# The first layer's selective scan as 256 time steps, with the sequences on the partitions

## The chip, the cores and the metric

The kernel runs on one core of one Trainium2 chip. The metric is the device time of the whole kernel in microseconds. Most executions of a kernel agree within 0.3%. A core has five engines with their own programs: TensorE (PE in the profile, with its weight loads as PEld), VectorE (DVE), ScalarE (ACT), GpSimd (POOL) and SyncE (SP, which here only starts transfers).

## The reference, cut to what matters

Two images of 64x64 positions and 256 channels go through two layers. Only the first is changed. It runs a selective scan over each image along both axes and in both directions, so there are 2 x 64 = 128 sequences of 64 steps for each axis and direction:

```python
xz = x @ in_proj_w.T                      # 256 -> 2 x 512
xi, z = jnp.split(xz, 2, axis=-1)
xi = silu(causal_conv(xi, 4 taps) + conv_b)
dt, Bm, Cm = jnp.split(xi @ x_proj_w.T, [DT_RANK, DT_RANK + D_STATE], axis=-1)
dt = softplus(dt @ dt_w.T + dt_b)
dA = jnp.exp(dt[..., None] * A)           # 512 channels x 16 states
dBu = (dt * xi)[..., None] * Bm[:, :, None, :]
def step(h, t):
    h = dA_t * h + dBu_t
    return (h, jnp.einsum('ndk,nk->nd', h, C_t))
y = (ys + xi * Dp) * silu(z)
return y @ out_w.T
# ... both directions and axes, then one product with fc_w, and the residual
```

The second layer (another kind of scan, with group norm) follows and is the same in both kernels.

## The kernel before

The channels lie on the partitions. A block is four sequences in both directions, and each block of each of the 16 states costs one pass of the hardware's scan instruction:

```python
for n in range(NS0):                      # 16 states
    for c in range(CT):                   # four groups of 128 channels
        nc.scalar.activation(decs[:, c, :, 1:], dts[:, c, :, 1:], AF.Exp, scale=neg_a[:, c, n:n+1])
    nc.vector.tensor_mul(h, dtx, b_n)     # b_n: row B_n on every partition, by a matmul
    nc.vector.tensor_tensor_scan(hf, decay_flat, hf, 0.0, ALU.mult, ALU.add)
    nc.vector.tensor_mul(h, h, c_n)       # c_n likewise
    ...                                   # the next block's front, in pieces
    for c in range(CT):                   # y += h * C, summed in PSUM
        nc.tensor.matmul(y[:, c, :], lhsT=k.ident, rhs=h[:, c, :], start=False, stop=n == NS0 - 1)
```

All numbers are float32 (f32).

## Time and profile before

| | time before |
|---|---|
| median of 3 runs | 14784.51 us (14781.2 to 14787.17) |
| layer 0 (two images) | 10,560 us |
| layer 1 (two images) | 4206 us |
| VectorE busy in layer 0 | 91% (9621 of 10,560 us) |
| TensorE busy in layer 0 | 86% (9105 of 10,560 us) |

These are two groups of instructions of the kernel before, shape by shape: line, engine, operation, out<-in, size, count, then busy us and the mean ns of one record, then idle time before them.

```profile
L379 PE MATMUL ps_y<-h,ident 128*128 128x512 f32 x8192 | 4363.8, 682 | 1052.1 <-DVE h L372 1041.1
...
L614 PE MATMUL ps_tr<-ident,xh 128*128 128x128 f32 x1024 | 155.0, 274 | 0.0
```

L379 is the last line of the code above. The kernel issues 64 blocks x 16 states x 4 = 4096 such products, and the profile has 8192 records. L614, a transpose in layer 1, is issued 1024 times and has 1024 records. So an f32 product leaves two records, and a transpose one.

### The profile page before, as it was taken

The page shows a single profiled execution, that of the slowest core. Times are in us where ns is not written, and L with a number is a line of the kernel's source. Part 1 is how long each engine was busy: PE and PEld are TensorE (multiplying, and loading weights), DVE is VectorE, ACT ScalarE, POOL GpSimd, SP SyncE. Part 2 cuts the span into 40 slices and gives each one's busy share as a digit, 9 for nine tenths or more (in the row PEclk, how much of TensorE's full clock was granted, in tenths as well). Part 3 has the DMA queues.
Part 4 walks back from the last instruction along what each step waited for, and adds up shares of the span by engine and source line. Part 5 has one row for each costly group of instructions (what it writes and reads, how often), then busy time and mean ns, then how long its engine had stood idle before and what let it go on. Part 6 is the DMA issues. An engine that isn't in the chain of part 4 may idle for free.

```text
span 14766.4 us, 110663 instructions
## 1 busy us (share of the span) xinstructions
PE 12671.3 (86%) x44688; PEld 6607.1 (45%) x44688; DVE 11979.4 (81%) x8514; ACT 6025.9 (41%) x8637; POOL 968.2 (7%) x1070
## 2 busy tenths in 40 slices
PE   8888888888888878888888888888888888788888
PEld 3433343434333345656533433334344333456565
DVE  8999999899999965555589999998999999655555
ACT  4444444444444423333344444444444444233333
POOL 0000000000000011111200000000000000111112
PEclk9999999999999989999989999989999998899999
DMA  0000000000000000000000000000000000000000
GB/s 18 0 0 0 0 0 6 0 0 0 0 0 0 0 10 5 1 6 3 15 13 0 0 0 0 0 6 0 0 0 0 0 0 0 10 6 1 6 4 9
DMA packets 23553, 46.87 MB, mean 3 GB/s; under 512 B 6592, under 2 KB 15296, under 8 KB 21504
## 3 DMA queue, kind: packets, MB, share of 16 engines
q1 hardware_dynamic: 23040, 39.80, 0.8%
q8 instruction: 350, 5.73, 0.2%
q14 instruction: 163, 1.34, 0.0%
HBM read 31.40 MB, written 8.39 MB: 3 GB/s over the span
## 4 chain that ended last, share of the span: by engine, by line
DVE 59%; PE 29%; ACT 8%; issue 3%; DMA 0%; POOL 0%; DVEq 0%; SPq 0%; POOLq 0%; ACTq 0%
DVE h L369 26%; DVE h L368 13%; DVE h L372 12%; PE ps_y L379 5%; PE ps_mm L530 5%; PE ps_mm L687 4%; PE ps_mm L403 3%; PE ps_mm L558 3%; DVE xn L508 2%; PE ps_y L672 2%; PE ps_seg L642 2%; PE ps_y L348 2%; ACT rms L450 2%; PE ps_bc L332 1%; PE ps_mm L242 1%
## 5 line engine op out<-in xcount | busy, mean ns | idle before, releaser
L379 PE MATMUL ps_y<-h,ident 128*128 128x512 f32 x8192 | 4363.8, 682 | 1052.1 <-DVE h L372 1041.1
L360 ACT ACTIVATE decay<-dt,neg_a 128x504 f32<-128x504 f32 x4096 | 2615.2, 704 | 5525.1 <-DVE h L369 5522.7
L369 DVE TENSOR_TENSOR_SCAN h<-decay,h 128x2048 f32<-128x2048 f32 x1024 | 4530.0, 4424 | 88.6 <-ACT xc L290 1.4
L379 PEld LDWEIGHTS ps_y<-h,ident 128*128 128x128 f32 x8192 | 1710.8, 219 | 3578.2 <-issue 1832.2
L372 DVE TENSOR_TENSOR h<-h,ps_bc 128x2048 f32<-128x2048 f32 x1024 | 2342.0, 2287 | 118.0 <-PE ps_bc L332 33.5
L332 PE MATMUL ps_bc<-dbc,ident 48*128 48x512 f32 x4096 | 2146.1, 637 | 305.1 <-DVE h L368 305.1
L368 DVE TENSOR_TENSOR h<-dtx,ps_bc 128x2048 f32<-128x2048 f32 x1024 | 2333.1, 2278 | 12.0 <-PE ps_bc L332 11.4
L530 PE MATMUL ps_mm<-xn,w_in 128*128 128x256 f32 (+1 forms) x5120 | 1388.1, 406 | 181.1 <-DVE xn L508 85.0
L332 PEld LDWEIGHTS ps_bc<-dbc,ident 48*128 48x128 f32 x4096 | 681.5, 189 | 1624.8 <-issue 1240.4
L530 PEld LDWEIGHTS ps_mm<-xn,w_in 128*128 128x128 f32 (+1 forms) x5120 | 873.3, 184 | 663.5 <-DVE xn L508 231.2
L687 PE MATMUL ps_mm<-yg,w_out 128*128 128x256 f32 x2048 | 527.9, 403 | 274.7 <-DVE conv L544 265.2
L224 POOL TENSOR_SCALAR xn<-XU,gn_scale,gn_shift 128x256 f32<-128x256 f32 x128 | 85.2, 676 | 8949.3 <-PE ps_mm L242 7097.7
L544 DVE SCALAR_TENSOR_TENSOR conv<-ps_mm,cols,conv 128x252 f32<-128x252 f32 (+2 forms) x1536 | 663.3, 467 | 9.3
L450 ACT ACTIVATE rms<-ps_mm,eps_rms 128x256 f32<-128x256 f32 x256 | 121.4, 474 | 1167.8 <-PE ps_mm L558 1167.8
L242 PE MATMUL ps_mm<-xn,w_in 128*128 128x256 f32 x2048 | 567.7, 425 | 21.9 <-ACT xi L251 21.9
L687 PEld LDWEIGHTS ps_mm<-yg,w_out 128*128 128x128 f32 x2048 | 381.1, 196 | 428.5 <-DVE conv L544 319.7
L360 ACT ACT_TABLE_LOAD x420 | 538.9, 1283 | 7.6
L242 PEld LDWEIGHTS ps_mm<-xn,w_in 128*128 128x128 f32 x2048 | 410.5, 209 | 221.7 <-issue 108.3
L403 PE MATMUL ps_mm<-h,w_out 128*128 128x256 f32 x2048 | 475.9, 385 | 27.8 <-DVE h L393 27.0
L508 DVE TENSOR_TENSOR xn<-XU,rms 128x256 f32<-128x256 f32 x256 | 278.5, 1126 | 251.9 <-ACT rms L450 251.9
L273 PE MATMUL ps_mm<-xi,diag_w 128*128 128x252 f32 (+2 forms) x1536 | 467.3, 385 | 0.0
L450 ACT ACTIVATE sq<-yg 128x1024 f32<-128x1024 f32 x128 | 135.3, 1057 | 808.2 <-DVE yg L679 808.2
(131 smaller groups left out, 11758.8 us busy)
## 6 DMA issues: line engine op xcount, KB each, us to landing
XU<-in_x_dram SPq DMA_DIRECT2D x16, 512.0 KB, 7.1
out_dram<-Y SPq DMA_DIRECT2D x32, 256.0 KB, 2.4
w_in<-in_L_t_Win_dram SPq DMA_DIRECT2D x4, 1160.0 KB, 5.1
w_in<-in_L_b_Win_dram SPq DMA_DIRECT2D x4, 1160.0 KB, 7.8
w_in<-in_L_mh_in_w_dram SPq DMA_DIRECT2D x2, 1024.0 KB, 7.9
dt<-in_L_fc_w_dram SPq DMA_DIRECT2D x4, 512.0 KB, 5.9
w_in<-in_L_mv_in_w_dram SPq DMA_DIRECT2D x2, 1024.0 KB, 4.8
w_out<-in_L_t_Wout_dram SPq DMA_DIRECT2D x4, 512.0 KB, 4.9
```

Of the source, the lines that this page charges most:

```text
L242: nc.tensor.matmul(pp[:, j * TB : (j + 1) * TB], lhsT=w_in[:, kt, mt * P : (mt + 1) * P], rhs=xn[:, kt, :], start=kt == 0, stop=kt == KT - 1,)
L332: nc.tensor.matmul(pb, lhsT=k.ident[:NX, r : r + 1].to_broadcast([NX, P]), rhs=dbc, start=True, stop=True,)
L360: nc.scalar.activation(decs[:, c, :, 1:], dts[:, c, :, 1:], AF.Exp, scale=neg_a[:, c, n : n + 1],)
L368: nc.vector.tensor_mul(h, dtx, b_n)
L369: nc.vector.tensor_tensor_scan(hf, decay.rearrange("p c v -> p (c v)"), hf, 0.0, ALU.mult, ALU.add)
L372: nc.vector.tensor_mul(h, h, c_n)
L379: nc.tensor.matmul(y[:, c, :], lhsT=k.ident, rhs=h[:, c, :], start=False, stop=n == NS0 - 1,)
L403: nc.tensor.matmul(po[:, o * TB : (o + 1) * TB], lhsT=w_out[:, c, j, o * P : (o + 1) * P], rhs=yg[:, c, j * TB : (j + 1) * TB], start=c == ...
L508: nc.vector.tensor_mul(seqs(xn[:, kt, :]), us[:, kt], seqs(rms))
L530: nc.tensor.matmul(ps, lhsT=w_in[:, kt, col : col + width], rhs=xn[:, kt, :], start=kt == 0, stop=kt == KT - 1,)
L544: nc.vector.scalar_tensor_tensor(dsts[:, :, j:], pss[:, :, : L - j], w[:, TAPS - 1 - j : TAPS - j], dsts[:, :, j:], ALU.mult, ALU.add,)
L687: nc.tensor.matmul(po[:, o * TB : (o + 1) * TB], lhsT=w_out[:, c, o * P : (o + 1) * P], rhs=yg[:, c, :], start=c == 0, stop=c == CT - 1,)
```

## The change

The intent is to take the scan instruction, and the broadcasts of B and C, away. Both images together have 128 sequences for one axis and direction, so the sequences go on the partitions, and the kernel steps through time itself: 2 axes x 2 directions x 64 = 256 steps, in 64 blocks of 4 steps. I call the four steps of a block n0 to n3. B and C are then per-partition scalars. The states are handled in pairs. The core of the new step:

```diff
-                    nc.vector.tensor_mul(h, dtx, b_n)
-                    nc.vector.tensor_tensor_scan(
-                        hf, decay.rearrange("p c v -> p (c v)"), hf, 0.0, ALU.mult, ALU.add
-                    )
-                    nc.vector.tensor_mul(h, h, c_n)
+                    if s % 2 == 0:
+                        e = two.tile([P, 4, DI], F32, name="e")
+                        nc.gpsimd.tensor_mul(
+                            e, w["a_bc"][s // 2], dt.unsqueeze(1).to_broadcast([P, 4, DI])
+                        )
+                    a = ps_a.tile([P, 2, DI], F32, name="ps_a")
+                    act(a, e[:, 2 * (s % 2) : 2 * (s % 2) + 2, :], AF.Exp)
+                run_late()                               # y of the pair before, see below
+                    nc.vector.tensor_mul(a, a, h)
+                for j in range(2):
+                        nc.vector.scalar_tensor_tensor(
+                            h[:, j, :], dtx, b_n, a[:, j, :], ALU.mult, ALU.add
+                        )
+                late.append(lambda s=s: sum_y(s))
+                pieces(s)                                # one piece of other blocks' work
```

y needs h turned back to channels on partitions. Even states do it by a product, odd ones by scaling and a transpose that adds into PSUM:

```diff
+YROUTE = ("diag", "act") * (NS0 // 2)
+                    if kind == "diag":
+                        dg = dgp.tile([P, TS], F32, name="dg")
+                        act(dg, k.ident, AF.Copy, scale=c_n)          # diagonal of C
+                        for c in range(CT):
+                            nc.tensor.matmul(y[:, c, :], lhsT=h[:, j, c * P : (c + 1) * P], rhs=dg, ...)
+                    else:
+                        hc = two.tile([P, DI], F32, name="hc")
+                        act(hc, h[:, j, :], AF.Copy, scale=c_n)       # (or GpSimd, not used here)
+                        for c in range(CT):
+                            nc.tensor.matmul(y[:, c, :], lhsT=hc[:, c * P : (c + 1) * P],
+                                rhs=k.ident, is_transpose=True, ...)
```

The work around the recurrence is cut in pieces that stand between the pairs s = 0 to 7 of a step:

```diff
+            def pieces(s, n=n, later=later, nxt=nxt):
+                flush()                    # evacuations of PSUM that are due, on ScalarE or VectorE
+                next(nxt, None)            # dt and dt*x of the next step
+                if n == 0:
+                    next(done, None)       # out_proj of the block before
+                if s >= 2:
+                    next(ahead, None)      # in_proj, conv, silu, x_proj of the next block
```

In effect out_proj and six of the eight pieces of in_proj fall in n0, the rest of in_proj and the conv in n1, the silu and x_proj in n2, and nothing in n3. A prologue writes the normalised x to DRAM in time order, the outputs go through DRAM too, and layer 1 is untouched. (The diff is cut, and lines are joined.)

## The prediction

> **What bounds the kernel now.** I read the split by stage first, then the page's chain and costliest groups, then VectorE's order of work, and at last single durations that the new code will repeat. The stage view gives, for each stretch in us, busy time of each engine (instructions), granted TensorE clock, DMA share and GB/s; I cut at the ends of layer 0 and layer 1 of each image.
>
> ```profile
> 0.00:5282.00 5282.00, 4548.79 (x10820) 2055.46 (x10820) 4810.89 (x1758) 2318.25 (x3221) 80.99 (x132) 0.92 0.01 2
> 5282.00:7384.00 2102.00, 1781.09 (x11524) 1246.76 (x11524) 1179.31 (x2502) 695.08 (x1098) 405.74 (x418) 0.97 0.02 7
> 7384.00:12662.00 5278.00, 4556.01 (x10820) 2055.91 (x10820) 4810.51 (x1757) 2317.49 (x3220) 76.23 (x104) 0.91 0.01 2
> 12662.00:14766.00 2104.00, 1785.38 (x11524) 1248.95 (x11524) 1178.66 (x2501) 695.12 (x1098) 405.24 (x416) 0.97 0.02 6
> ```
>
> Layer 0 is 5282 + 5278 = 10,560 us, layer 1 is 4206. In layer 0 VectorE is busy 91%, ScalarE 44%, GpSimd 1.5%. The chain says the same:
>
> ```profile
> DVE 59%; PE 29%; ACT 8%; issue 3%; DMA 0%; POOL 0%; DVEq 0%; SPq 0%; POOLq 0%; ACTq 0%
> ...
> L369 DVE TENSOR_TENSOR_SCAN h<-decay,h 128x2048 f32<-128x2048 f32 x1024 | 4530.0, 4424 | 88.6 <-ACT xc L290 1.4
> ...
> L372 DVE TENSOR_TENSOR h<-h,ps_bc 128x2048 f32<-128x2048 f32 x1024 | 2342.0, 2287 | 118.0 <-PE ps_bc L332 33.5
> ...
> L368 DVE TENSOR_TENSOR h<-dtx,ps_bc 128x2048 f32<-128x2048 f32 x1024 | 2333.1, 2278 | 12.0 <-PE ps_bc L332 11.4
> ```
>
> Each of the 1024 (64 blocks of sequences x 16 states) pays scan 4.42 + two products 2.28 each = 9.0 us on VectorE: 9205 us of the 10,560. VectorE idles little before any of them. The scan costs 2.16 ns per element, twice a product. So layer 0 is VectorE's; TensorE's 86% is work beside it.
>
> **The Trainium skill.** (1) "SBUF — State Buffer", Who interferes with whom: a VectorE instruction with two SBUF inputs contends with a GpSimd one that reads SBUF, one with at most one SBUF input does not. The trace agrees (min/median/max ns):
>
> ```profile
> L508 DVE TENSOR_TENSOR xn<-XU,rms x256: 414/1259/1322, 5310.3 to 14712.6; 128x256 f32<-128x256 f32 x128
> L618 DVE TENSOR_TENSOR xdt<-ps_tr,dt x256: 673/682/692, 5335.0 to 14745.6; 128x512 f32<-128x512 f32 x128
> ```
>
> L508 reads two SBUF tiles and triples where a GpSimd instruction runs; L618 reads PSUM and SBUF, half of its 256 fall beside GpSimd, and none moves. (2) "GPSIMD Engine Reference", Elementwise: 4497 ns for a product of 2048 f32. Here a 128x512 product took 1.04 us (L641) to 1.27 (L706), so 4.2 to 5.1 for 2048; agrees. (3) "TensorE: Matmul & The Clock Gate", Part 1: the clock is halved after an idle window of about 3.4 us and given back after a busy one. The trace has 400 half-speed stretches, 2048 us in all; counting streaming time in 3.4 us windows, 116 of 120 full-speed windows under 40% lead to half speed, and half speed ends only after windows of 70% or more. (4) "ScalarE: Activation LUTs", What ACT_TABLE_LOAD costs: back-to-back ACTIVATEs overlap by about 93 ns; here four 704 ns exponentials take 2.53 us, so each next one costs 0.61.
>
> **The change.** Layer 1 is the same: 4206 us stay. Layer 0 now handles both images together, 128 sequences on the partitions: 2 axes x 2 directions x 64 = 256 time steps, in 64 blocks of 4. The scan is gone: the recurrence is an ordinary product and sum, so each state element costs VectorE two element passes, not four (scan counts twice). B and C are per-partition scalars, so their broadcasts (4096 matmuls) go, and C leaves VectorE altogether. GpSimd takes dt*A, ScalarE one large exponential to PSUM. Every VectorE product has one operand in PSUM, so I expect no port contention.
>
> VectorE, per pair of states: product 128x1024, PSUM and SBUF: 1.22 us (the same size took 1225 ns in L393). Two scalar_tensor_tensor 128x512 with a pointer scalar: L544 took 0.471 at 252 elements and 0.463 at 244, 1 ns per element and 0.21 fixed, so 0.74 each. Order of work shows +0.11 us before a dependent instruction and -0.08 (overlap) before an independent one:
>
> ```profile
> 1062.43 2.29 DVE L372 TENSOR_TENSOR h<-h,ps_bc 128x2048 f32<-128x2048 f32 x1
> 1064.67 2.29 DVE L368 TENSOR_TENSOR h<-dtx,ps_bc 128x2048 f32<-128x2048 f32 x1
> 1067.06 4.42 DVE L369 TENSOR_TENSOR_SCAN h<-decay,h 128x2048 f32<-128x2048 f32 x1
> 1071.59 2.29 DVE L372 TENSOR_TENSOR h<-h,ps_bc 128x2048 f32<-128x2048 f32 x1
> ```
>
> Sum 1.22 + 1.48 - 0.05 = 2.65; eight pairs 21.2 us. Softplus end, dt*x and gate: three of 0.69 (L618's size) = 2.1; output sums two of 0.7 per block, 0.35 per step. **VectorE 23.65 us per step, 94.6 per block.**
>
> ScalarE: per pair exponential 1.06, diagonal of C 128x128 0.39 (L360's slope), scaled h 128x512 0.71; less 0.09 overlap each, 1.88; eight are 15.0. Softplus, three dependent of 512: 1.9. Per block 12 evacuations of 0.57 to 0.68, two silu of 2048 (1.95), two table loads of 1.28 and smaller ones: 16, or 4 per step. About 21 us.
>
> TensorE at full clock, start to start: 0.111 us for 128 columns (12 of L662 in 1.60 us, the last's length included), 0.109 for a transpose (L614), 0.43 for 512. Per step 72 of 128 columns 8.0, dt 0.43, and per block in_proj 6.9, conv 6.9, x_proj 1.7, output 3.4, or 4.8 per step: 13.2 us. By this a diagonal and a transposed state cost TensorE the same.
>
> GpSimd: four products of 2048 at 4.2 to 5.1: 17 to 20 us.
>
> So VectorE stays the bound of a step, with ScalarE at 88% of it. Not everything hides, because ScalarE runs in program order and only two PSUM buffers of decays exist. In an ordinary pair, from h done: scaled h 0.62, one evacuation 0.48, next exponential 1.06, hand-overs 0.1 = 2.26 < 2.65, so VectorE is fed. Softplus (1.9) is mostly met by VectorE's own dt work. But the two silu with their loads, 6.5 us in one place, leave VectorE dry for about 5.4 us per block. TensorE streams 9/24 = 37% in the block's fourth step and 45% in its third, so by the rule above it drops to half clock and meets the next block's output and in_proj products (0.85 each then) cold; ScalarE and VectorE wait for these. Estimate 4 us per block, and 1.5 for the rest. **Block: 94.6 + 5.4 + 4 + 1.5 = 105.5; 64 blocks are 6752 us.**
>
> Around it: a prologue normalises x and writes it by time to DRAM, 16.8 MB in 256-byte runs. Packets of 216, 368 and 768 bytes took 14, 22 and 36 ns on an engine, so about 17 for 256: 65,536 / 16 x 17 = 70 us, mostly exposed since layer 0's memory is the prologue's. With load, statistics (21 us to the first matmul before), weights, A spread and the first block's front: 190 us, none of it overlapped. Axis change: weights, A and front again in series, 75. Last output 15. Gathering y from DRAM, 8.4 MB per image in 256-byte runs, 35 us plus 10 of adds: 90 for both.
>
> Sum: 190 + 6752 + 75 + 15 + 90 + 4206 = 11,328; I say **11,350 us**, ratio 0.77.
>
> **Rivals.** (a) *VectorE saturated*: front work hides wholly; 94.6 x 64 = 6054, total about 10,630. For it: ScalarE's slack per pair. Against: strict order and the 6.5 us silu. (b) *ScalarE or TensorE takes over*: TensorE at half clock needs 26.4 us per step, over VectorE's 23.65, and each evacuation then waits for its product; the mixed route for y suggests that neither engine had room to spare. At 30 us per step, 7680, total 12,260. For it: 37% load in the fourth step. Against: a half-clock TensorE saturates in the first two steps and so earns its clock back. (c) *GpSimd and VectorE lock each other out*, if the pointer scalar counts as an SBUF input: 17 us of lock beside 12 us of scalar_tensor_tensor per step, some 36 us per step and 13,800. L544 never falls beside GpSimd here, so the trace cannot exclude it; the page and L618 speak against it. (d) *Small DRAM runs*: three times the time makes 210 us more, 11,560.
>
> **Range and chances.** Only (c) with another loss gets near 14,500. (a) sets the low side, (b) with part of (d) the high one: 10,850 to 12,200. Faster by over 2%: 0.97; within: 0.02; slower: 0.01.
>
> **What would show it.** In the steps VectorE about 90% busy, ScalarE about 80%, GpSimd 65 to 80%, TensorE's clock clearly under the 0.92 of before; 105 us per block; 1.22 and 0.74 us for the two VectorE forms, unchanged beside GpSimd; one gap of about 5 us per block at the table loads. Wrong if VectorE under 80% in the steps (ScalarE or TensorE bound), if the 0.74 us form stretches beside GpSimd, or if more than 300 us pass before the first step.

## The result, and the profile after

The kernel after takes 12317.76 us (12307.46 to 12321.38, 3 runs). The ratio to the kernel before is 0.8331, with a 95% interval of 0.8316 to 0.8345. It is faster, but 968 us slower than predicted and 118 us over the predicted range.

The page after, its chain (shares of the span that end last) and its costliest groups:

```profile
PE 51%; DVE 23%; ACT 22%; issue 3%; SPq 1%; DMA 1%; POOL 0%; ACTq 0%; DVEq 0%; POOLq 0%
...
L492 POOL TENSOR_TENSOR e<-a_bc,dt 128x2048 f32<-128x2048 f32 x1008 | 4585.6, 4552 | 3261.8 <-ACT ps_a L226 2217.7
L499 DVE TENSOR_TENSOR ps_a<-ps_a,h 128x1024 f32<-128x1024 f32 x2016 | 2475.8, 1228 | 1662.3 <-ACT ps_a L226 1640.6
...
L506 DVE SCALAR_TENSOR_TENSOR h<-dtx,bc,ps_a 128x512 f32<-128x512 f32 x4032 | 2840.6, 743 | 73.6 <-PE ps_y L474 0.5
L460 PE MATMUL ps_y<-dg,h 128*128 128x128 f32 x16384 | 2368.5, 289 | 546.2 <-ACT dg L226 528.9
...
L474 PE MATMUL ps_y<-ident,hc 128*128 128x128 f32 x8192 | 1302.3, 283 | 81.4 <-ACT hc L226 81.4
```

Three things are to be seen. First, the chain has passed from VectorE (59% before) to TensorE (51%). Second, the durations on VectorE are those predicted: 1.228 us for the product and 0.743 for the scalar form, on the same page as GpSimd's 4.552. But VectorE idles 1640.6 us before L499, for an exponential on ScalarE. Third, L460 and L474 do the same number of operations (256 steps x 8 states x 4 = 8192 each), and the diagonal's products have twice the records.

Where the time goes within a block is seen by cutting one block (the 20th) at the starts of the four gate products. The columns are the stretch in us and its length, then busy time (and count) of PE, PEld, DVE, ACT, POOL, then the granted clock, DMA share and GB/s.

```profile
2622.20:2657.79 35.59, 33.01 (x150) 20.44 (x150) 24.12 (x31) 20.42 (x34) 18.18 (x5) 0.95 0.08 30
2657.79:2691.94 34.15, 31.44 (x174) 23.03 (x174) 22.64 (x29) 20.71 (x34) 18.24 (x5) 1.00 0.05 16
2691.94:2721.18 29.24, 20.91 (x122) 14.01 (x122) 22.54 (x29) 24.36 (x34) 18.13 (x5) 0.94 0.00 1
2721.18:2744.68 23.50, 17.56 (x110) 14.24 (x110) 22.34 (x28) 17.31 (x28) 18.22 (x5) 0.93 0.00 1
```

VectorE has some 22 to 24 us of work in each of the four. Only n3 lasts no longer than that. In n0 and n1 TensorE is busy 93% and 92%. The medians of all such steps are 35.59, 34.15, 29.26 and 23.51 us, 122.5 together, against 105.5 predicted. The two steps with in_proj, conv and out_proj hold it all: 69.7 us, where the prediction leaves 105.5 - 29.05 (VectorE's 23.65 and the 5.4 of the silu gap) - 23.65 = 52.8.

Within n0, the order of work of ScalarE, VectorE and TensorE (start, length, and the idle time before with its releaser in brackets):

```profile
2642.09 0.60 ACT L226 ACTIVATE xi<-ps_mm 128x512 f32<-128x512 f32 x1 [0.60 <-PE ps_mm L339]
2642.58 1.02 ACT L226 ACTIVATE ps_a<-e 128x1024 f32<-128x1024 f32 x1
```

```profile
2643.64 1.23 DVE L499 TENSOR_TENSOR ps_a<-ps_a,h 128x1024 f32<-128x1024 f32 x1 [0.37 <-ACT ps_a L226]
2644.90 1.40 DVE L506 SCALAR_TENSOR_TENSOR h<-dtx,bc,ps_a 128x512 f32<-128x512 f32 x2
2646.68 1.23 DVE L499 TENSOR_TENSOR ps_a<-ps_a,h 128x1024 f32<-128x1024 f32 x1 [0.37 <-ACT ps_a L226]
```

```profile
2640.16 1.88 PE L339 MATMUL ps_mm<-xn,w_in 128*128 128x512 f32 x4
2641.88 1.05 PE L460 MATMUL ps_y<-dg,h 128*128 128x128 f32 x8
2642.78 0.60 PE L474 MATMUL ps_y<-ident,hc 128*128 128x128 f32 x4
2643.21 1.88 PE L339 MATMUL ps_mm<-xn,w_in 128*128 128x512 f32 x4
```

A pair takes 3.04 us (2643.64 to 2646.68 on VectorE), though VectorE works only some 2.65. TensorE has no gap: one piece of in_proj is two products, which are four records, start to start 1.72 us (2640.16 to 2641.88), and y takes 1.33 (2641.88 to 2643.21), 3.05 in all. ScalarE's program has the evacuation xi ahead of the next exponential, xi waits 0.60 for TensorE's product, and VectorE then waits 0.37 for the exponential. So a wait that the profile puts down to ScalarE has its cause in TensorE.

From here on I count "streaming", the time for which TensorE has to take in columns: records in a stretch times the start-to-start spacing of one record at full clock, 0.429 us for 512 columns, 0.216 for 256, 0.109 for 128. It is independent of how long a record is shown, and of a slower clock. For the block above it is 29.74, 29.79, 16.19 and 12.59 us for n0 to n3, 88.3 in all or 22.1 per step. The prediction had 13.2.

### The profile page after: what moved, and what is told of

Its sections match the earlier page's. It is cut to its first block, busy times and chain, and to the rows that moved or that the text cites. A ratio compares the mean times of both kernels' runs of the same rounds, so it can differ in the third digit from the quotient of the medians. Undisturbed runs are those within 1.5% of the kernel's fastest.

```text
span 12319.7 us, 149295 instructions
## 1 busy us (share of the span) xinstructions
PE 10205.8 (83%) x58864; PEld 7129.2 (58%) x58864; DVE 8281.0 (67%) x12184; ACT 6703.2 (54%) x10283; POOL 5424.8 (44%) x1910
## 4 chain that ended last, share of the span: by engine, by line
PE 51%; DVE 23%; ACT 22%; issue 3%; SPq 1%; DMA 1%; POOL 0%; ACTq 0%; DVEq 0%; POOLq 0%
DVE h L506 8%; PE ps_mm L339 7%; PE ps_mm L368 7%; PE ps_y L460 7%; DVE ps_a L499 7%; PE ps_mm L747 5%; PE ps_mm L904 4%; PE ps_mm L550 4%; ACT ps_a L226 4%; ACT tmp L226 4%; PE ps_mm L775 3%; ACT hc L226 3%; PE ps_y L474 3%; PE ps_mm L385 3%; PE ps_seg L859 2%
## 5 line engine op out<-in xcount | busy, mean ns | idle before, releaser
L492 POOL TENSOR_TENSOR e<-a_bc,dt 128x2048 f32<-128x2048 f32 x1008 | 4585.6, 4552 | 3261.8 <-ACT ps_a L226 2217.7
L499 DVE TENSOR_TENSOR ps_a<-ps_a,h 128x1024 f32<-128x1024 f32 x2016 | 2475.8, 1228 | 1662.3 <-ACT ps_a L226 1640.6
L460 PEld LDWEIGHTS ps_y<-dg,h 128*128 128x128 f32 x16384 | 2123.5, 198 | 1337.3 <-ACT dg L226 761.5
L506 DVE SCALAR_TENSOR_TENSOR h<-dtx,bc,ps_a 128x512 f32<-128x512 f32 x4032 | 2840.6, 743 | 73.6 <-PE ps_y L474 0.5
L460 PE MATMUL ps_y<-dg,h 128*128 128x128 f32 x16384 | 2368.5, 289 | 546.2 <-ACT dg L226 528.9
L226 ACT ACTIVATE hc<-h,bc 128x512 f32<-128x512 f32 x2048 | 1467.3, 716 | 1081.6 <-DVE h L506 964.7
L226 ACT ACTIVATE ps_a<-e 128x1024 f32<-128x1024 f32 x2016 | 2041.7, 1013 | 0.7
L474 PE MATMUL ps_y<-ident,hc 128*128 128x128 f32 x8192 | 1302.3, 283 | 81.4 <-ACT hc L226 81.4
L474 PEld LDWEIGHTS ps_y<-ident,hc 128*128 128x128 f32 x8192 | 962.1, 144 | 230.0 <-ACT hc L226 173.0
L339 PE MATMUL ps_mm<-xn,w_in 128*128 128x512 f32 x2048 | 989.1, 602 | 126.5 <-DVE dt L416 126.5
```

What stands on the lines that cost most here:

```text
L226: tc.keep_in_program_order(nc.scalar.activation(*args, **kwargs))
L339: nc.tensor.matmul(pp, lhsT=w["w_in"][:, kt, mt * P : (mt + 1) * P], rhs=xn[:, kt, :], start=kt == 0, stop=kt == KT - 1,)
L460: nc.tensor.matmul(y[:, c, :], lhsT=h[:, j, c * P : (c + 1) * P], rhs=dg, start=False, stop=stop and c == CT - 1,)
L474: nc.tensor.matmul(y[:, c, :], lhsT=hc[:, c * P : (c + 1) * P], rhs=k.ident, is_transpose=True, start=False, stop=stop and c == CT - 1,)
L492: nc.gpsimd.tensor_mul(e, w["a_bc"][s // 2], dt.unsqueeze(1).to_broadcast([P, 4, DI]))
L499: nc.vector.tensor_mul(a, a, h)
```

## The experiments

Ten kernels ran. A is the theory that TensorE, with two records for each product, holds n0 and n1; B its rival of that run. The texts quote means over the blocks, which are up to 1 us from the sums of medians here. Runs with one time are read by their step medians and by differences far over 0.3%. The median of n0 hides two kinds: in the kernel after, 37 of the 62 ordinary n0 (the first block and the change of axis left out) have one stretch of 3.41 us in which TensorE's clock is halved, and last 35.59 us in the median; the 25 others have none, and last 33.90. Other kernels have it in another number of blocks, so that their medians of n0 can differ by 1.7 us for this alone: it is in 1 of 62 in all_diag, in none in load_in_last_step and half_front, in 28 in no_silu, and in 36 in spread. The kernel before took 14777.08 us beside the first four, 14786.62 (7 runs) beside the next three and 14782.34 (7 runs) beside the last three.

| kernel | n0 | n1 | n2 | n3 | sum | total us |
|---|---|---|---|---|---|---|
| after | 35.59 | 34.15 | 29.26 | 23.51 | 122.5 | 12317.76 |
| all_diag | 35.65 | 35.06 | 26.62 | 22.47 | 119.8 | 12185.94 |
| all_transpose | 31.41 | 31.40 | 29.90 | 23.34 | 116.1 | 11937.45 |
| load_in_last_step | 32.89 | 34.15 | 29.25 | 36.80 | 133.1 | 12982.94 |
| half_front (wrong result) | 28.39 | 27.14 | 30.17 | 23.50 | 109.2 | 11491.28 |
| no_silu (wrong result) | 33.93 | 34.14 | 23.49 | 23.50 | 115.1 | 11914.96 |
| spread | 28.32 | 30.34 | 30.87 | 23.50 | 113.0 | 11728.81 |
| spread_t12 | 27.70 | 26.64 | 31.72 | 23.14 | 109.2 | 11480.95 |
| spread_t16 | 25.65 | 25.61 | 30.15 | 23.37 | 104.8 | 11280.13 |
| spread_pool2 | 29.90 | 26.93 | 31.15 | 26.98 | 115.0 | 11894.71 |
| spread_pool4 | 29.26 | 28.52 | 32.19 | 26.07 | 116.0 | 12003.63 |

### All states by the diagonal

```diff
-YROUTE = ("diag", "act") * (NS0 // 2)
+YROUTE = ("diag",) * NS0
```

> All 16 states of y by products with a diagonal of C. Theory A (an f32 product is two passes and two records of TensorE, so a diagonal state costs it 0.87 us and a transposed one 0.44; TensorE sets the first two steps of each block of four): TensorE streams 3.5 us more per step, the two long steps of a block go from 35.5 and 33.9 us to about 39 and 37.5, the last step stays at 23.5; about +7 us per block of 64, total 12,700 to 12,850. Theory B (the in-order ScalarE is what lengthens the steps, TensorE has room): ScalarE is relieved of 8 x 0.31 us per step, so total 12,000 to 12,320.

Measured: 12185.94 us, correct. The total is a miss for theory A: it fell. But the middle pairs of n0 behave as A says. This is ScalarE's order of work there:

```profile
2603.58 0.60 ACT L226 ACTIVATE xi<-ps_mm 128x512 f32<-128x512 f32 x1 [1.38 <-PE ps_mm L339]
2604.07 1.02 ACT L226 ACTIVATE ps_a<-e 128x1024 f32<-128x1024 f32 x1
2605.02 0.68 ACT L226 ACTIVATE dg<-ident,bc 128x128 f32<-128x128 f32 x2
2607.08 0.60 ACT L226 ACTIVATE xi<-ps_mm 128x512 f32<-128x512 f32 x1 [1.38 <-PE ps_mm L339]
```

A pair now takes 3.50 us, and its streaming is 16 x 0.109 + 4 x 0.429 = 3.46; in the kernel after it was 12 x 0.109 + 1.72 = 3.03 of 3.05. ScalarE waits 1.38 us for the product instead of 0.60, although it has less to do. So TensorE sets the pair. The step did not grow by as much, because n0 of the kernel after is 5.85 us (35.59 - 29.74) longer than its streaming, outside the middle pairs (which are full), and n0 of all_diag only 2.1 (35.65 - 33.54). Of the difference, 1.7 us is the half clock that all_diag lacks: between n0 at full clock the step grew by 1.75 (33.90 to 35.65). The expectation A overlooked that n0 is not filled by TensorE from end to end. The fall of n2 by 2.6 us fits ScalarE's relief of 8 x 0.33 (a diagonal costs it 0.39 us, a scaled h 0.72), but no run isolates it. Why n3 fell by 1.0 I did not look into.

### All states by the transpose

```diff
-YROUTE = ("diag", "act") * (NS0 // 2)
+YROUTE = ("act",) * NS0
```

> All 16 states of y by scaling and transposes. Theory A: TensorE streams 3.5 us less per step, but ScalarE needs 2.5 us more, so that a pair with an evacuation becomes ScalarE's at about 2.9 us against 3.05 now; 2 to 5 us less per block, total 12,000 to 12,200. Theory B: 2.5 us more of ScalarE in each of the three long steps, total 12,700 to 12,800.

Measured: 11937.45 us, correct. This is further than A expected (6.4 us less per block, where it said 2 to 5), and in the opposite direction to B. ScalarE has 2.6 us more work per step (8 x 0.33), and n0 and n1 still fall by 4.2 and 2.8 us. Streaming falls by 3.48 us in each step, which is 8 states x 4 x 0.109: one record saved per operation. "A diagonal and a transposed state cost TensorE the same" is refuted, and B, by which ScalarE's extra work would lengthen the steps, too. n0 and n1 stay well above their streaming of 26.3, so the amount of TensorE's work is not all.

### Products in the step that has none

```diff
             def pieces(s, n=n, later=later, nxt=nxt, blk=blk):
+                if n == NB - 1 and s >= 2:
+                    idle = mm()
+                    for q in range(CT):       # four products of 512 columns, not read
+                        nc.tensor.matmul(idle, lhsT=k.ident, rhs=blk["xc"][:, q, :], ...)
```

> In the last step of each block, the only one at VectorE's 23.5 us, four f32 products of 512 columns that nobody reads are added to TensorE in six of its eight pairs; ScalarE and VectorE get nothing. Theory A: such a pair streams 1.31 + 3.43 = 4.74 us against VectorE's 2.65, so the step becomes about 36 us, +12 us per block, total about 13,100. If an f32 product of 512 columns cost 0.43 us, as predicted, a pair would stream 0.66 + 1.72 = 2.4 us and hide: total 12,320. Theory B: no change either, 12,320.

This measures the disputed cost by itself: 24 products of 512 columns in n3, read by no other engine. Counted as the prediction did, they add 24 x 0.43 = 10.3 to a streaming of 12.59: 22.9 us, hidden under VectorE's 23.5. Counted as two records each, they make 33.2. Measured: n3 36.80, total 12982.94, correct. TensorE in n3:

```profile
2944.97 0.60 PE L474 MATMUL ps_y<-ident,hc 128*128 128x128 f32 x4
2945.41 3.60 PE L619 MATMUL ps_mm<-xc,ident 128*128 128x512 f32 x8
2948.84 1.05 PE L460 MATMUL ps_y<-dg,h 128*128 128x128 f32 x8
```

The four products written above appear as x8 and take 3.43 us, start to start (2945.41 to 2948.84): 0.86 us a product. A is confirmed, and so is the unit. The next n0 is 2.7 us shorter, which gives back part of the loss: 1.7 of it is the half clock, which no n0 of this run has (0 of 62, against 37). The rest I did not follow.

### Half of the front's products

```diff
-                for kt in range(KT):              # in_proj: two products per piece
+                # one product per piece
-                for j in range(1, TAPS):          # conv: four taps
+                for j in range(1, 2):             # two taps
```

> Wrong results on purpose: half of the products of in_proj and half of the conv columns are left out, with all evacuations, silu and their order kept. Theory A: TensorE streams 5 us less in a block's first step and 8.5 less in its second; about 11 us less per block, total 11,500 to 11,800. Theory B: the number and order of ScalarE's instructions is the same, so under 2% less, above 12,070.

Its output is wrong, which doesn't matter for the time. Measured: 11491.28 us (relative error 0.668). This is just below A's range and far from B's. n0 and n1 fall by 7.2 and 7.0 us, for 5.2 and 8.6 us less streaming; 1.7 of n0's fall is the half clock, which no n0 has here. All of VectorE's and ScalarE's instructions are still there, so these 14 us belong to TensorE's front products. n2 grows by 0.9, and n3 is untouched.

### No silu

```diff
-            act(gate, gate, AF.Silu)
-            act(xc, xc, AF.Silu)
-            tc.keep_in_program_order(nc.scalar.preload_act_table_set(LOG_EXP))
```

> Wrong results on purpose: the two silu of 2048 elements per block and their two table loads are left out of layer 0's steps. Both theories: the third step of a block, 29.4 us now, falls by the 5.4 us that the prediction gave to this gap, to about 24; the others stay; total about 11,970. If the gap is made by the products around it and not by the 6.5 us on ScalarE: less than 2 us per block, above 12,190.

Measured: 11914.96 us (relative error 1.89). Its output is wrong, which doesn't matter for the time. n2 falls from 29.26 to 23.49, by 5.8 us, and becomes like n3; n1 stays, and so does n0: its median is 1.7 us lower only because fewer blocks have the half clock (28 of 62), while the two lengths, 33.90 and 35.59, are the same. So the gap of the silu and its table loads, predicted at 5.4 us, is real, and it is all that n2 has over VectorE's own work.

### Front and back spread evenly

```diff
-        def front(blk):
+        def front(blk, between=()):
+                if mt == CT:
+                    yield from between            # out_proj of the block before, in the middle of in_proj
-                pc = mm(lambda pc: act(xc[:, c, :], pc, AF.Identity, bias=bias))
+                pc = mm()                         # conv, x_proj, out_proj: in two halves,
+                    if n == 3:                    # the evacuation queued after the second
+                        yield
+                taking.append(lambda pc=pc: act(xc[:, c, :], pc, AF.Identity, bias=bias))
-                if n == 0:
-                    next(done, None)
-                if s >= 2:
-                    next(ahead, None)
+                next(ahead, None)                 # one piece in each pair, from s = 0
```

(The diff is cut.)

> The same instructions, but the front of the next block and the output products of the last one are cut in units of about 1.7 us of TensorE and dealt one to each of the 24 pairs of a block's first three steps, instead of whole pieces to 15 of them. Theory A: each pair streams 1.31 + 1.72 = 3.03 us, so steps of about 26.4, 26.4, 29 (with the silu) and 23.5, 105 us per block against 122.8; total 11,100 to 11,350. Theory B: the same number of instructions in ScalarE's order, so within 2%, 12,070 to 12,560.

Measured: 11728.81 us (11723.64 to 11730.77, 4 runs), ratio 0.7933 (0.7921 to 0.7944), correct. The streaming of a block is the same 88.3 us, now 24.17, 28.70, 21.57 and 13.87. The block is 9.5 us shorter with the work of TensorE, ScalarE and VectorE unchanged. (The evacuations also move in ScalarE's program, so the 9.5 is not TensorE's placement alone.) The expectation was too hopeful: n1 and n2 keep 30.3 and 30.9. In n1 TensorE still streams 28.7.

### Spread, and fewer diagonals

```diff
-YROUTE = ("diag", "act") * (NS0 // 2)
+YROUTE = ("diag", "act", "act", "act") * (NS0 // 4)   # spread_t12; spread_t16: ("act",) * NS0
```

> As spread, with 4 of 16 states by the diagonal and 12 by transposes. Theory A: TensorE streams 1.75 us less per step, ScalarE gets 1.25 more; steps of about 25, 25, 28.5 and 23.5, 102 per block, total 10,850 to 11,200. Theory B: slower than spread by the extra ScalarE work, by 1.25 x 192 = 240 us.

Measured: 11480.95 us (11472.38 to 11487.87, 4 runs), ratio 0.7767 (0.7754 to 0.778), correct; better than spread, but again short of what I expected.

> Theory A (TensorE streams two passes for every f32 product and one for a transpose, so each state that goes from the diagonal to the scaled transpose saves it 0.44 us and costs ScalarE 0.33): against spread_t12 four more states per step save TensorE 7.0 us per block and cost ScalarE 5.2. Step medians n0 26.5, n1 25.5, n2 32.5 (ScalarE holds it, so it grows), n3 23.3; block about 107.8, total about 11,370. Theory B (TensorE is no longer what holds n0 and n1 in this order; the scheduling of ScalarE does): n0 and n1 stay at 27.7 and 26.6 or grow, n2 grows by 1 or more, total 11,500 or more.

Measured: 11280.13 us (11278.63 to 11288.86, 4 runs), ratio 0.7633 (0.762 to 0.7646), correct. This is the best version. It beats both kernels, and A's expectation by 90 us. n0 and n1 come down to 25.6, within 2.3 us of n3. One part of A failed: n2 did not grow to 32.5 under ScalarE's extra work, but fell from 31.72 to 30.15. The windows of its block, cut as for the kernel after:

```profile
2285.84:2310.93 25.09, 24.25 (x107) 15.59 (x108) 23.66 (x30) 21.28 (x31) 17.86 (x4) 0.90 0.01 3
2310.93:2336.79 25.86, 25.69 (x129) 16.74 (x128) 22.73 (x27) 23.22 (x35) 18.26 (x4) 1.00 0.17 60
2336.79:2367.21 30.42, 23.51 (x116) 14.29 (x114) 22.47 (x27) 27.99 (x35) 18.24 (x4) 0.89 0.00 0
2367.21:2390.56 23.35, 16.97 (x78) 12.07 (x78) 22.45 (x29) 20.35 (x29) 18.51 (x5) 0.77 0.00 1
```

VectorE is busy 94% of n0, 88% of n1 and 96% of n3, so it is near the bound again that it was predicted to be. Only n3 is clearly its own: TensorE is busy 97% of n0 and 99% of n1 (in n1 it streams 24.4 of the 25.86 us). In n2 ScalarE is busy 92%. That step's gap stands in VectorE's order of work:

```profile
2348.72 1.41 DVE L514 SCALAR_TENSOR_TENSOR h<-dtx,bc,ps_a 128x512 f32<-128x512 f32 x2
2356.40 1.23 DVE L507 TENSOR_TENSOR ps_a<-ps_a,h 128x1024 f32<-128x1024 f32 x1 [6.27 <-ACT ps_a L226]
```

and its cause in ScalarE's, where the exponential at 2355.34 follows the silu:

```profile
2349.03 1.28 ACT L226 ACT_TABLE_LOAD   x1
2350.32 1.91 ACT L226 ACTIVATE gate<-gate 128x2048 f32<-128x2048 f32 x1
2352.14 1.89 ACT L226 ACTIVATE xc<-xc 128x2048 f32<-128x2048 f32 x1
2354.05 1.28 ACT L383 ACT_TABLE_LOAD   x1
2355.34 1.03 ACT L226 ACTIVATE ps_a<-e 128x1024 f32<-128x1024 f32 x1
```

### Some states scaled on GpSimd

```diff
-YROUTE = ("diag", "act") * (NS0 // 2)
+YROUTE = (("act",) * 7 + ("pool",)) * (NS0 // 8)      # spread_pool2; spread_pool4: 3 and 1, (NS0 // 4)
```

> As spread_t16, but the scaled h of two of the 16 states comes from GpSimd (one 128x512 product by a pointer scalar, estimated 1.1 us from the 4.55 us of 128x2048). A: ScalarE is relieved by 1.4 us per step, GpSimd goes from 18.2 to 20.4 us per step and stays under VectorE's 23.5; n2 falls by 1 to 2 us against spread_t16, the others stay: block 106 to 107, total 11,260 to 11,330. B: GpSimd runs in order, so its decay product of the next pairs waits behind the scaled h of this pair, and VectorE waits for it: steps 24.5 or more in n3, total above spread_t16.

Measured: 11894.71 us (11884.93 to 11904.64, 4 runs), ratio 0.8047 (0.8035 to 0.8059), correct. B holds: n3 26.98, and the total is 615 us above spread_t16. Groups of this kernel, shape by shape:

```profile
L500 POOL TENSOR_TENSOR e<-a_bc,dt 128x2048 f32<-128x2048 f32 x1008 | 4592.0, 4558 | 1959.6 <-ACT ps_a L226 1811.0 <-DVE dt L424 148.3 <-POOL e L500 0.2
L482 PE MATMUL ps_y<-ident,hc 128*128 128x128 f32 x16384 | 2741.0, 308 | 965.0 <-POOL hc L480 632.2 <-ACT hc L226 326.3
...
L480 POOL TENSOR_SCALAR hc<-h,bc 128x512 f32<-128x512 f32 x512 | 803.8, 1570 | 110.0 <-PE ps_y L482 66.8 <-ACT hc L226 41.8 <-POOL e L500 1.1
```

One scaled h takes GpSimd 1.57 us where I had estimated 1.1, and TensorE waits 632.2 us for it. GpSimd's work per step is 18.2 + 2 x 1.57 = 21.4 us, under the 26.98 that n3 lasts. So it is not its amount of work; what is left is the waiting in order, of GpSimd and of TensorE behind it.

> As spread_pool2 with four of 16 states on GpSimd: 18.2 + 4 x 1.1 = 22.6 us per step, with waits in order close to VectorE's 23.5. A: n3 becomes GpSimd's at 24 to 26 us, and the total is 11,300 to 11,500. B (GpSimd's order does not matter): n3 stays at 23.5, n2 at 29 to 30, total about 11,150.

Measured: 12003.63 us, correct; both theories had expected less. n3 is 26.07 with 18.2 + 4 x 1.57 = 24.5 us of GpSimd's work. Which of the waits in order (for h, for one of the two buffers of the scaled h, behind a 4.55 us decay product) costs most, these two runs don't tell apart.

## Why the prediction was right or wrong

**What failed: "TensorE at full clock ... 13.2 us", and with it "By this a diagonal and a transposed state cost TensorE the same".** The spacings of 0.111, 0.109 and 0.43 us were right, but they are those of a record, and I multiplied them by the number of products. An f32 product is two records. Everything but the transposes was halved: in_proj costs 13.7 us per block, not 6.9, conv 13.8, not 6.9, x_proj 3.4, not 1.7, out_proj 6.9, not 3.4, and a diagonal state 0.87, a transposed one 0.44. The product alone, in the last step, measures 0.86 us for 512 columns. The counts of the kernel before (8192 records for 4096 products) would have told it. So would the Trainium skill's "FP8 and Floating Point Precision", TensorE Precision Notes, which I did not consult: it gives true FP32 four passes. With the 215.7 ns start to start at N = 512 and full clock of "TensorE: Matmul & The Clock Gate", Part 1, that makes 0.863 us per product, an estimate from these two pages; measured 0.86.

**What took its place.** TensorE's mean of 22.1 us per step is still under VectorE's 23.65. The work is uneven, though: 29.7 us in n0 and in n1. So rival (b), which I had set at a half-clock TensorE, came true with the clock at 0.95, and its 12,260 us, got from the wrong reason, is near the 12317.76. Of the 17.0 us by which the block was mis-sized, spread takes off 9.5 by placing the same work evenly, and changing the diagonals to transposes another 8.2 (113.0 to 104.8). Together they bring the block to 104.8, beside the 105.5 predicted. The two remedies are together as large as the miss, but that 104.8 lies beside 105.5 is partly luck: TensorE still streams 18.6 us per step there, and not 13.2.

**"4 us per block for a cold clock" was right in kind and too large.** It costs 1.7 us in each of the 37 of 62 n0 that have it (35.59 us against 33.90), so about 1.0 us per block. In the block shown the clock is halved from 2628.18 to 2631.59, on the output products, as predicted:

```profile
2627.12 5.40 PE L550 MATMUL ps_mm<-gate,w_out 128*128 128x512 f32 x8 [2.04 <-DVE dt L416]
2632.36 1.05 PE L460 MATMUL ps_y<-dg,h 128*128 128x128 f32 x8
```

Eight records take 5.24 us, start to start, where the full clock gives 3.43. The stretch before it streams 34% (TensorE idles 2.04 us in it, by the profile for VectorE's dt). n3 as a whole streams 12.59 of 23.5 us, which is 54%, and not 37%: here too the count was halved. So the granted clock was not "clearly under the 0.92 of before": it is 0.953, and 0.93 in n3. In spread_t16 n3 streams 10.4 of 23.35, 45%, and the clock there does fall, to 0.77. It costs n3 nothing visible, as VectorE is busy 96% there. In n0 of that kernel the clock is 0.90; what this costs was not isolated. The prediction's own count of clock windows ("116 of 120") I could not repeat: over the whole profile before, 269 of 285 full-speed windows under 40% are followed by half speed, and 399 of the 400 half-speed stretches end after a window of 70% or more. The rule stands.

**VectorE's 23.65 us per step was right.** n3, which has nothing else in it, lasts 23.51 us. The single durations hold: 1.228 us (1.22 predicted), 0.743 (0.74), GpSimd 4.552 (4.2 to 5.1; the 4497 ns that the prediction quotes from the skill for a product is that page's figure for an addition). "VectorE stays the bound of a step" holds for n3 alone. VectorE is busy 75% of the block shown (91.64 of 122.48 us) and not 90%, so the prediction's own sign, "Wrong if VectorE under 80% in the steps", came true.

**Rival (c), locking of GpSimd and VectorE, fell.** GpSimd's products take over 18 us of each step. Of the 4032 scalar_tensor_tensor of VectorE, 3460 run beside a GpSimd instruction, with a median of 0.742 us; the other 572 have 0.743.

**"The two silu ... leave VectorE dry for about 5.4 us" was right.** Removing them shortens n2 by 5.8.

**ScalarE's order was right in kind, with a wrong term.** "In an ordinary pair ... 2.26 < 2.65, so VectorE is fed" took the evacuation as ready. It waits for its product, 0.60 us in each middle pair of n0.

**The rest of the sum held.** The first step begins at 187.6 us (the first start of L504); the prediction had 190. The interval with the change of axis is 96 us, for 75 plus one step of some 25. From the last gate, at 8010.1, to the end of the profiled span at 12319.7 there are 4310 us; predicted 15 + 90 + 4206 = 4311. Rival (d), slow DRAM runs, has no room in this.

## What to carry to other kernels

Before multiplying a duration by a count, divide the profile's records by the operations that the source issues; for f32 products the quotient is two here, for transposes one, so a product with a diagonal costs TensorE twice a transpose. Compare the engines' work step by step and not by the mean of a block, since an engine that is busy 83% on average can be the bound of half the steps. Look also at whether a step's lengths are of one kind before you quote their median: here n0 had two, 1.7 us apart, by the clock. And when a wait names one engine, look at what stands ahead of the awaited instruction in that engine's program: here an evacuation that waited for TensorE stood ahead of an exponential for VectorE.

## What the Trainium skill lacked or had wrong

- "FP8 and Floating Point Precision", TensorE Precision Notes: it is right that true FP32 costs four passes in time, but neither it nor "Perfetto Trace Analysis" (whose section Engine Utilization halves TensorE's rate for FP32_LOW_HIGH in a footnote) says how this stands in a profile: two MATMUL records for each product, 0.429 us start to start for 512 columns, 0.86 for the product.
- "TensorE: Matmul & The Clock Gate", Part 4: it gives some 275 ns for a (bf16) transpose in a kernel's context, and says that the full clock does not engage for transposes. The records here are as long (274 and 283 ns on average), but an f32 transpose of 128x128 starts 0.109 us after the one before it, which is the figure to multiply. And f32 transposes do hold the full clock: in all_transpose, of the 3.41 us windows at full clock in which TensorE streams nothing else, all 62 with 40 to 50% of transposes keep it (such as 267.94 to 271.36: 15 records, all of L474, clock 1.00 in it and in the next), and 188 of 190 with 10 to 40% lose it. Three windows at half clock that they fill by over 90% give it back.
- "TensorE: Matmul & The Clock Gate", Part 1: it gives the window, but not how much streaming in a window counts as busy. In the kernel after, cut in windows of 3.41 us at the clock's own changes, all 105 full-clock windows with under 30% of streaming are followed by half clock, 105 of 182 between 30 and 40%, and 21 of 2949 above. Half clock ends after 228 of 232 windows of 80% or more, and after 3 of 105 of less. Over whole steps, 54% of streaming had a clock of 0.93, 45% had 0.77, and 39% (n3 of all_transpose, 9.12 of 23.34 us) had 0.65.
- "GPSIMD Engine Reference", Engine selection: it says that one-input operations run at roughly the line rate on GpSimd. A product of 128x512 by a per-partition scalar took 1.57 us, which is 3.1 ns per element, more than two-input products: 1.04 to 1.27 us at the same size (L641 and L706 of the kernel before), 2.2 ns per element at 2048 (4552 ns).
